# Second layer: expert weights kept in SBUF, eight row buffers for nine, shared places for short tiles

## The chip, the cores and the metric

The kernel runs on one core of a Trainium2 chip. The metric is the device time of one execution in microseconds (us), the median over several runs. Engines are named as in the profile: PE (matmul) with PEld (its weight loads), DVE (vector), ACT (scalar), POOL (GpSimd) and SP (used here as a queue for DMAs).

## The reference

A graph network of two layers on 3125 nodes of 256 features and 100000 edges sorted by destination. Each layer adds to `x` a neighbour part and an attention part, then an expert part. The change concerns the second layer, which is this:

```python
xn = _layernorm(x, axis=-1)
x = x + _L1_gnn_ref(xn, W, attn_src, attn_dst, edge_index, edge_type) + _L1_mix_ref(xn[None], ...)[0]
x = x + _L1_ffn_ref(_layernorm(x, axis=-1)[None], ...)[0]

# _L1_gnn_ref: 8 relations, 8 heads of 32
h_all = einsum('nf,rof->rno', x, W).reshape(r, n, h, d)
h_src = h_all[edge_type, src]; h_dst = h_all[edge_type, dst]
scores = leaky_relu(h_src . attn_src + h_dst . attn_dst, 0.2)
w = exp(scores - max(segment_max(scores, dst), 0)[dst])
w = w / (segment_sum(w, dst) + 1e-12)[dst]
out = segment_sum(h_src * w, dst)

# _L1_mix_ref: k, v normalized per head
kv = einsum('bhsd,bhse->bhde', k, v) / S
out = (q @ kv) @ wo.T + bo

# _L1_ffn_ref: 6 experts of three 256x256 layers, the two best per node
rh = relu(f @ router_w1 + router_b1); p = softmax(rh @ router_w2 + router_b2)
h1 = relu(f @ expert_w1 + b1); h2 = relu(h1 @ expert_w2 + b2); y = h2 @ expert_w3 + b3
out = sum over the two best of softmax weight * y
```

## The kernel before

Everything up to about 1500 us is the first layer and is not touched. Then come two stages of the second layer.

**The table stage** (L2263 to L2361, about 1504 to 1788 us): for each of 25 tiles of 128 nodes, the rows `y` of the first layer's experts are gathered, the node is normalized, and its products with the weights of all 8 relations are written to a table in DRAM (`tab`, rows of 264 numbers: 256 features and 8 scores); `kv` is summed up on the side. The loads of this stage are issued by SP at its start: `wq`, `wo` and `bo` of the attention part, then `wt` (2 MB), `wkv` and smaller ones.

**The attention and expert stage** (class `Layer1`, 1787 us to the end) has one order of work written out by hand: the instructions of each engine run in the order of the program (`manual_schedule`). The edges are cut into 25 blocks, 24 of 34 x 128 edges and one of 15 x 128. `run` goes through them:

- `gather(b)` fetches the table rows of a block into row tiles `r` of 7 edges per partition, five tiles a block (7, 7, 7, 7, 6), by one indirect DMA of POOL per edge column (L1383). The tiles come from the pool `at_r`, which has nine buffers: a tile takes the place of the one nine before it, when PE has summed that one.
- `start(b)` issues the place data (`a3`, `mk`, `m4` on ACT's queue, in `places`) and the edge lists `oe`, five chunks of 256 KB (on SP's queue, `load`), compares a chunk into one-hots `ot` on DVE (`turn`, L1203), and picks the destination scores by matmul (`pick`, L1214); `own` (L1225) reduces them on DVE. This is done for block b+2 at the end of block b and spread through block b+1. `oe` and `ot` have three buffers each.
- `block(b)` adds the scores (`raw`, L1402; it needs all five row tiles), takes the maximum over a node's edges by scans (DVE, with a transpose `lp` on PE, a copy `ls` on ACT, L1417, and the way back), the exponential on ACT (L1444), then for each row tile multiplies rows by weights on DVE (L1454), builds the one-hots `oh` (L1457) and sums by matmul (`sums`, L1468). The sum of a block is closed in the next block (`close`, L1486 and on), normalized and turned into `xt` for the experts.
- The experts work on groups of blocks (`TOGETHER`: five groups of four, one of three, one of two). A group's work is a generator, `group`, whose units PE, ACT and DVE take piece by piece at set points of a block (`take(us)`). The three weights of each expert are loaded in every group again, a few experts ahead, by SP (`weights` through `load_k`, L352), into tiles with two buffers for each of the three layers:

```python
for i, n in ((1, e + 2), (2, e + 2), (3, e + 1)):
    self.weights(ws, i, n)
```

- `mix`, ahead of block 0, makes one matrix of `kv`, `wq` and `wo` and adds the attention part to all 25 tiles, reading back the normalized nodes (`xt`, 512 KB a load, two buffers, L1554).

What a queue holds is served in order: an issue on SP that waits for a free place holds up all that SP issues later.

Of the kernel before, what the change touches and what calls it, by code (L numbers as in the profile page):

```python
# [7 lines left out]
F32 = mybir.dt.float32  # L8
BF = mybir.dt.bfloat16
# [4 lines left out]
PSUM = bass.MemoryType.PSUM  # L14
DRAM = bass.MemoryType.DRAM

N, D, E = 3125, 256, 100000
P = 128
# [15 lines left out]
NE1 = 6  # L34
R, HD, DH = 8, 8, 32
# [872 lines left out]
CW = 8  # L908
# [226 lines left out]
class Layer1:  # L1135
# [3 lines left out]

    def __init__(self, tc, C, a, out, one, wk, rows, ps, B, table, apart, x1t, mixed, xs):  # L1140
        self.tc, self.nc, self.C, self.a, self.out = tc, tc.nc, C, a, out
        self.one, self.wk, self.rows, self.ps = one, wk, rows, ps
        self.B, self.table, self.apart, self.xs = B, table, apart, xs
        self.x1t, self.mixed = x1t, mixed
        nc = tc.nc
        t = lambda shape, dt, name: one.tile(shape, dt, name=name)
        self.ones = t([1, P], F32, "l1_ones")
        nc.vector.memset(self.ones, 1.0)
        self.carry = [t([HD, 2, P], F32, f"carry{i}") for i in range(2)]
        for x in self.carry:  # L1150
            nc.vector.memset(x, -BIG)
        self.down = t([P, NE1], F32, "l1_down")
        nc.vector.tensor_scalar(self.down, C.row[:, :NE1], -1.0, float(NE1), op0=OP.mult, op1=OP.add)
        ld = lambda shape, name, src: (t(shape, F32, name), src)
        loads = [ld([NE1, D], "b3", a["L1_ffn_expert_b3"]),
                 ld([P, NE1, 2], "bc1", a["L1_ffn_expert_b1c"]), ld([P, NE1, 2], "bc2", a["L1_ffn_expert_b2c"]),
                 ld([P, NE1], "rw2", a["L1_ffn_router_w2"]), ld([P, 1], "rb1", a["L1_ffn_router_b1c"]),
                 ld([P, NE1], "rb2", row_bc(a["L1_ffn_router_b2"], NE1))]
        for x, src in loads:
            nc.sync.dma_start(x, src)  # L1160
        self.b3, self.bc1, self.bc2, self.rw2, self.rb1, self.rb2 = (x for x, _ in loads)
        self.rw1 = load_k(nc, one, a["L1_ffn_router_w1"], "rw1")
        self.late = []
        self.stores = []
        self.units = iter(())
        self.queue = []
# [19 lines left out]
    def load(self, A, c):  # L1186

        if c >= A["n"]:
            return
        k = min(CW, A["w"] - c * CW)  # L1190
        i = A["c0"] + c * CW
        oe = self.wk.tile([P, CW * P], BF, name="oe", bufs=3)
        self.nc.sync.dma_start(oe[:, :k * P], self.B.order[i:i + k, :].rearrange("c e -> (c e)")[None, :]
                               .to_broadcast([P, k * P]))
        A["oe"][c] = oe

    def turn(self, A, c):

        if c >= A["n"]:
            return  # L1200
        k = min(CW, A["w"] - c * CW) * P
        ot = self.wk.tile([P, CW * P], BF, name="ot", bufs=3)
        self.nc.vector.tensor_scalar(ot[:, :k], A["oe"].pop(c)[:, :k], self.C.p, None, op0=OP.is_equal)  # L1203
        A["ot"][c] = ot
# [13 lines left out]
    def own(self, A, c):  # L1218
        nc = self.nc
        if c >= A["n"]:  # L1220
            return
        k = min(CW, A["w"] - c * CW)
        s = slice(c * CW, c * CW + k)
        own = self.wk.tile([P, CW, HD, R], F32, name="own")
        nc.vector.tensor_tensor(own[:, :k], A["dp"].pop(c)[:, :k],  # L1225
                                A["orel"][:, s, None, :].to_broadcast([P, k, HD, R]), OP.mult)
        nc.vector.tensor_reduce(A["ad"][:, s, :], own[:, :k], AX.X, OP.add)  # L1227
# [17 lines left out]

    def weights(self, ws, i, e):
        if e < NE1:
            ws[i, e] = load_k(self.nc, self.wk, self.a[f"L1_ffn_expert_w{i}"][e], f"ew{i}")

    def group(self, t0, nt, xt):  # L1250
# [4 lines left out]
        bc = lambda x: x[:, :, None].to_broadcast(sh)  # L1255
        ws = {}
        for i, e in ((1, 0), (1, 1), (2, 0), (3, 0), (2, 1)):
            self.weights(ws, i, e)

        rp = ps.tile([P, 512], F32, name="hp", bufs=2)  # L1260
        for j in range(2):
            nc.tensor.matmul(rp[:, :W], self.rw1[:, j, :], xt[:, j, :W], start=(j == 0), stop=(j == 1))  # L1262
        rh = wk.tile([P, 512], F32, name="rh", bufs=1)
        nc.scalar.activation(rh[:, :W], rp[:, :W], AF.Relu, bias=self.rb1)
# [10 lines left out]
        h1, h2 = {}, {}  # L1275
# [68 lines left out]
        for e in range(NE1):  # L1344
# [9 lines left out]
            for i in range(nt):  # L1354
# [4 lines left out]
                yield 0.9  # L1359
            for i, n in ((1, e + 2), (2, e + 2), (3, e + 1)):  # L1360
                self.weights(ws, i, n)
            self.store()
# [27 lines left out]
    def block(self, b, part, A, N):  # L1390
# [3 lines left out]
        mk, m4 = A["mk"], A["m4"]  # L1394
        keep = wk.tile([P, 2, HD, w + 2], F32, name="kp", tag=f"kp{w}", bufs=1)
        for i in range(2):
# [4 lines left out]
        for s0, k, r, _ in part:  # L1401
            nc.vector.tensor_tensor(raw[:, s0:s0 + k, :], A["ad"][:, s0:s0 + k, :], r[:, :k, D:], OP.add)  # L1402
        sc = wk.tile([P, HD, w + 2], F32, name="sc", tag=f"sc{w}")
        inner = sc[:, :, 1:w + 1]
# [3 lines left out]
        for i in range(2):  # L1408
            t = wk.tile([P, HD, w], F32, name="tm", tag=f"tm{w}", bufs=1)
            nc.vector.tensor_tensor(t, inner, m4[:, 3 - i, None, :w].to_broadcast([P, HD, w]), OP.add)  # L1410
            nc.vector.tensor_reduce(lf[:, i, :], t, AX.X, OP.max)
# [23 lines left out]

        mx = wk.tile([P, 2, HD, w + 2], F32, name="mx", tag=f"mx{w}", bufs=1)
        f = lambda x: x.rearrange("p h c -> p (h c)")
# [14 lines left out]
        for q, (s0, k, r, got) in enumerate(part):  # L1452
# [3 lines left out]
            i = c0 + s0  # L1456
# [21 lines left out]
    def close(self):  # L1478
# [8 lines left out]
        nc.vector.reciprocal(den, den)  # L1487
        y = wk.tile([P, HD, DH], F32, name="y")
        nc.vector.tensor_tensor(y, sp[:, :D].rearrange("p (h d) -> p h d", h=HD),
# [40 lines left out]
    def mix(self):  # L1530

        nc, wk, ps, xs = self.nc, self.wk, self.ps, self.xs
        cx, wq, wo, bo = self.mixed
        ct = wk.tile([P, 2, P], F32, name="ct", tag="x1")
# [43 lines left out]
    def run(self):  # L1578
# [10 lines left out]
        for b in range(NB):  # L1589
            ahead = self.gather(b + 1) if b + 1 < NB else None  # L1590
            self.block(b, part, A, N)
            part, A = ahead, N
            N = self.start(b + 2) if b + 2 < NB else {"n": 0}
            self.store()
# [480 lines left out]
def fast(ctx: ExitStack, tc: tile.TileContext, a, out, flag):  # L2075
# [192 lines left out]
    with tc.tile_pool(name="n1", bufs=1) as n1:  # L2268
        apart = dram.tile([NB, P, 3, HD * R], BF, name="apart")
        x1t = dram.tile([(NB + 3) // 4, P, 2, 512], F32, name="x1t")  # L2270
        cx = n1.tile([P, 2, P], F32, name="cx1")
        wq = load_k(nc, n1, a["L1_mix_wqT"], "wq")
        wo = load_k(nc, n1, a["L1_mix_woT"], "wo")
        bo = n1.tile([1, D], F32, name="bo")
# [89 lines left out]
        with tc.tile_pool(name="at_1", bufs=1) as one, tc.tile_pool(name="at_w", bufs=2) as wk, \  # L2364
                tc.tile_pool(name="at_r", bufs=9) as rows, tc.tile_pool(name="at_p", bufs=1, space=PSUM) as ps:
            with tc.manual_schedule():
                Layer1(tc, C, a, out, one, wk, rows, ps, B_, tab2, apart, x1t, (cx, wq, wo, bo), xs).run()

# [60 lines left out]
```

## Time and profile before

| what | value |
|---|---|
| time, median of 3 runs | 3158.33 us (3147.89 to 3163.19) |
| the profiled execution | 3159.71 us, span 3157.9 us |
| busy: PE, DVE, POOL, ACT | 83%, 56%, 35%, 23% of the span |
| mean granted clock of PE | 0.907 |
| row gathers, L1383 | 831, 1105 ns each |
| `sums` matmuls, L1468 | 1662, 411 ns each |
| row multiplications, L1454 | 123, 1953 ns each |
| loads of expert weights, L352 | 126 of 256 KB |
| loads of edge lists, L1193 | 97 of 256 KB, 25 shorter |
| HBM read, written | 321.04 MB, 97.96 MB |

How to read it: shares of busy time are means over stages with different limits. A line such as "POOL r L1383 <- PE tp L1524: 25.4, 5, 8.9" in the list of waits says that POOL's instructions of line 1383, which write tile `r`, waited for that PE instruction 25.4 us in total, 5 times, 8.9 us at the longest. In a timeline each row is: start in us, length in us, engine, line, operation, what it writes and reads, shapes, how many; in the bracket, the idle time of the engine before it and what ended that. An engine's name with a q (SPq, ACTq) is its queue issuing a DMA. A releaser is inferred: the instruction named came last before the start.

### The profile page before, as it was taken

How to read it: one execution, taken by the hardware profiler on the slowest of the kernel's cores; microseconds unless marked ns; L12 is line 12 of the kernel's file. 1: busy time of each engine (PE TensorE's matmuls, PEld its weight loads, DVE VectorE, ACT ScalarE, POOL GpSimd, SP SyncE). 2: the span in 40 equal slices, each digit the busy share in tenths (PEclk: the TensorE clock that was granted, in tenths of full speed). 3: DMA queues.
4: the chain of work that ended last, by engine and by line, in shares of the span. 5: the costliest groups of instructions: out<-in, count | busy, mean ns of one | idle time of the engine just before them, and what ended most of it. 6: DMA issues, size and time to landing. Idle time of an engine off the chain costs nothing. (4 is left out here: it accounts for less than half of the span.)

```text
span 3157.9 us, 38213 instructions
## 1 busy us (share of the span) xinstructions
PE 2610.1 (83%) x13696; PEld 1774.8 (56%) x13696; DVE 1752.6 (56%) x3882; ACT 737.6 (23%) x1637; POOL 1113.6 (35%) x1040
## 2 busy tenths in 40 slices
PE   2667789999992999999699785397887877878878
PEld 1455544454562888888344354355555555555656
DVE  7777754444664111111676557566777667766652
ACT  3333402212231222222222101122121222212122
POOL 2000000001116500000600267777777777767700
PEclk9887999999995999999899887689898898898989
DMA  3555432223323665645643444445555555545512
GB/s 110 148 154 158 125 93 73 74 77 95 109 81 96 203 195 186 200 148 168 192 132 128 146 139 121 137 139 146 142 147 146 141 141 146 148 127 155 147 40 85
DMA packets 382415, 421.68 MB, mean 134 GB/s; under 512 B 143879, under 2 KB 316045, under 8 KB 381959
## 3 DMA queue, kind: packets, MB, share of 16 engines
q1 hardware_dynamic: 311680, 270.61, 28.5%
q0 software_dynamic: 49072, 132.49, 14.9%
q10 hardware_dynamic: 21462, 16.03, 1.7%
q8 instruction: 110, 1.80, 0.2%
q14 instruction: 91, 0.74, 0.1%
HBM read 321.04 MB, written 97.96 MB: 133 GB/s over the span
## 5 line engine op out<-in xcount | busy, mean ns | idle before, releaser
L1383 POOL DMA_INDIRECT r<-tab,b_at x831 | 918.6, 1105 | 498.5 <-issue 230.9
L1468 PE MATMUL sums<-r,oh 128*128 128x264 f32 x1662 | 423.6, 411 | 43.3 <-DVE oh L1457 24.8
L1468 PEld LDWEIGHTS sums<-r,oh 128*128 128x128 f32 x1662 | 334.1, 203 | 126.4 <-issue 50.7
L1909 POOL DMA_INDIRECT route_x<-x,slot x50 | 50.3, 1007 | 869.2 <-DVE slot L1905 722.8
L1454 DVE TENSOR_TENSOR r<-r 128x1792 f32<-128x1792 f32 (+2 forms) x123 | 240.2, 1953 | 0.0
L2184 PE MATMUL agg<-at,px 128*128 128x512 bf16 (+2 forms) x1050 | 237.4, 357 | 2.2 <-DMA at<-adj 2.2
L2030 PE MATMUL fhp<-fxe,fw 128*128 128x256 f32 x1024 | 233.9, 387 | 0.8 <-DVE fxe L2015 0.6
L2038 PE MATMUL fyp<-fw,fhid 128*128 128x256 f32 x1024 | 226.3, 379 | 0.0
L1322 PE MATMUL yp<-ew,h 128*128 128x256 f32 x600 | 163.8, 424 | 68.9 <-DVE xs L1326 68.9
L2184 PE MATMUL agg<-at,py 128*128 128x512 bf16 (+4 forms) x1200 | 216.4, 333 | 0.0
L2030 PEld LDWEIGHTS fhp<-fxe,fw 128*128 128x128 f32 x1024 | 188.1, 193 | 40.7 <-ACT fhid L2031 6.3
L2301 POOL DMA_INDIRECT y<-route_y,slot x50 | 50.3, 1005 | 452.9 <-DMA wq<-in_L_mix_wqT 429.0
L2038 PEld LDWEIGHTS fyp<-fw,fhid 128*128 128x128 f32 x1024 | 192.1, 190 | 24.8
L1273 ACT ACTIVATE h<-hp,bc 128x512 f32<-128x512 f32 (+2 forms) x168 | 106.2, 639 | 421.4 <-PE hp L1270 421.4
L2320 PE MATMUL hp<-wt,xt 128*128 128x512 f32 x400 | 183.3, 607 | 8.9 <-DVE stage L2323 5.6
L2031 ACT ACTIVATE fhid<-fhp,fb 128x256 f32<-128x256 f32 x256 | 121.1, 473 | 290.8 <-PE fhp L2030 267.2
L1322 PEld LDWEIGHTS yp<-ew,h 128*128 128x128 f32 x600 | 122.3, 213 | 105.7 <-DVE xs L1326 81.6
L1214 PE MATMUL dp<-a,ot 128*128 128x64 bf16 x2493 | 109.1, 206 | 82.5 <-DVE own L1225 45.9
L1634 PE MATMUL cnt<-oh_s,oh_a 128*125 128x128 bf16 x1250 | 99.3, 240 | 88.2 <-ACT adj_o L1635 60.6
L1270 PE MATMUL hp<-xt,ew 128*128 128x512 f32 (+2 forms) x336 | 158.3, 597 | 13.9 <-ACT h L1273 12.3
L1634 PEld LDWEIGHTS <-oh_a 128*125 128x125 bf16 x1250 | 96.1, 155 | 125.7 <-issue 75.2
L1214 PEld LDWEIGHTS <-ot 128*128 128x128 bf16 x2493 | 104.0, 106 | 104.7 <-issue 48.6
(418 smaller groups left out, 3858.6 us busy)
## 6 DMA issues: line engine op xcount, KB each, us to landing
fw<-in_L_ffn_W SPq DMA_DIRECT2D x64, 1024.0 KB
ew<-in_L_ffn_expert_w SPq DMA_DIRECT2D x126, 256.0 KB
at<-adj SPq DMA_DIRECT2D x44, 640.0 KB
route_x<-zero SPq DMA_DIRECT2D x104, 256.0 KB
tab<-stage SPq DMA_DIRECT2D x25, 1056.0 KB
oe<-b_order SPq DMA_DIRECT2D x97, 256.0 KB
adj<-adj_o SPq DMA_DIRECT2D x78, 250.0 KB
r<-tab,b_at POOLq DMA_INDIRECT x831
```

Source lines behind the costliest of these rows:

```text
L1214: nc.tensor.matmul(dp[:, i, :, :].rearrange("p h r -> p (h r)"), ot[:, i * P:(i + 1) * P], A["a3"][:, j, :], start=(j == 0), stop=(j == 2))
L1270: nc.tensor.matmul(hp[:, :W], ws[i, e][:, n, j * P:(j + 1) * P], x[:, n, :W], start=(n == 0), stop=(n == 1))
L1322: nc.tensor.matmul(yp, h2[e][:, n, i * P:(i + 1) * P], ws[3, e][:, n, :], start=(n == 0), stop=(n == 1))
L1383: st = self.nc.gpsimd.indirect_dma_start(out=r[:, c, :], out_offset=None, in_=self.table, in_offset=bass.IndirectOffsetOnAxis(ap=self.B.at ...
L1454: nc.vector.tensor_tensor(rv, rv, r[:, :k, D:, None].to_broadcast([P, k, HD, DH]), OP.mult)
L1468: mm = nc.tensor.matmul(self.sums, oh[:, c, :], r[:, c, :], start=(i == 0), stop=(i == w - 1))
L1634: nc.tensor.matmul(cnt[:, i, :], a[:, o, :M], s[:, o, :], start=(h == 0), stop=(h == 1))
L2030: nc.tensor.matmul(hp, w1[:, k, i * P:(i + 1) * P], xe[:, k, :], start=(k == 0), stop=(k == 1))
L2031: nc.scalar.activation(hid[:, i, :], hp, AF.Gelu, bias=b1[:, 0, i:i + 1])
L2038: nc.tensor.matmul(yp, hid[:, i, t * P:(t + 1) * P], w2[:, i, :], start=(i == 0), stop=(i == K1 - 1))
L2184: nc.tensor.matmul(agg[g][:, :cw], parts[j][:n, k, g * P:(g + 1) * P], at[:n, i, :cw], start=(k == 0 and j == 0), stop=(k == NB - 1 and j ...
L2320: nc.tensor.matmul(hp.rearrange("p r d -> p (r d)"), xt[:, k, :], wt[:, k, j * 512:(j + 1) * 512], start=(k == 0), stop=(k == 1))
```

## The change

- The weights of the six experts (18 tiles of 256 KB, 2 KB a partition) get places of their own in the pool of single buffers (`at_1`) and are loaded once: two experts after each of blocks 0, 1 and 2. `group` only reads them, and `weights` is gone.
- The row pool `at_r` has eight buffers for nine. `oe` and `ot` have two for three, `own` and `y` one for two.
- The tiles `kp`, `sc`, `tm` and `mx`, which had places apart for the short last block, use those of the full blocks; `rh` takes a place of `h2`.
- `wq` and `wo` are no longer loaded with the table stage's weights but at the start of `Layer1`, into the two places of `xt`; the constant `l1_ones` is replaced by a row of one that exists.

```diff
-        self.ones = t([1, P], F32, "l1_ones")
-        nc.vector.memset(self.ones, 1.0)
+        self.ones = ones[:1, :]
...
         self.rw1 = load_k(nc, one, a["L1_ffn_router_w1"], "rw1")
+        self.wq, self.wo = (wk.tile([P, 2, D], F32, name=n, tag="xt") for n in ("wq", "wo"))
+        for x, n in ((self.wq, "wq"), (self.wo, "wo")):
+            nc.sync.dma_start(x, a[f"L1_mix_{n}T"].rearrange("(k p) n -> p k n", p=P))
+        self.ws = {}
...
-        oe = self.wk.tile([P, CW * P], BF, name="oe", bufs=3)
+        oe = self.wk.tile([P, CW * P], BF, name="oe", bufs=2)
...
-        ot = self.wk.tile([P, CW * P], BF, name="ot", bufs=3)
+        ot = self.wk.tile([P, CW * P], BF, name="ot", bufs=2)
...
-        own = self.wk.tile([P, CW, HD, R], F32, name="own")
+        own = self.wk.tile([P, CW, HD, R], F32, name="own", bufs=1)
...
-    def weights(self, ws, i, e):
-        if e < NE1:
-            ws[i, e] = load_k(self.nc, self.wk, self.a[f"L1_ffn_expert_w{i}"][e], f"ew{i}")
-
     def group(self, t0, nt, xt):
...
-        ws = {}
-        for i, e in ((1, 0), (1, 1), (2, 0), (3, 0), (2, 1)):
-            self.weights(ws, i, e)
+        ws = self.ws
...
-        rh = wk.tile([P, 512], F32, name="rh", bufs=1)
+        rh = wk.tile([P, 2, 512], F32, name="rh", tag="h2")[:, 0, :]
...
-            for i, n in ((1, e + 2), (2, e + 2), (3, e + 1)):
-                self.weights(ws, i, n)
             self.store()
...
-        keep = wk.tile([P, 2, HD, w + 2], F32, name="kp", tag=f"kp{w}", bufs=1)
+        keep = wk.tile([P, 2, HD, w + 2], F32, name="kp", bufs=1)
...
-        sc = wk.tile([P, HD, w + 2], F32, name="sc", tag=f"sc{w}")
+        sc = wk.tile([P, HD, w + 2], F32, name="sc")
...
-            t = wk.tile([P, HD, w], F32, name="tm", tag=f"tm{w}", bufs=1)
+            t = wk.tile([P, HD, w], F32, name="tm", bufs=1)
...
-        mx = wk.tile([P, 2, HD, w + 2], F32, name="mx", tag=f"mx{w}", bufs=1)
+        mx = wk.tile([P, 2, HD, w + 2], F32, name="mx", bufs=1)
...
-        y = wk.tile([P, HD, DH], F32, name="y")
+        y = wk.tile([P, HD, DH], F32, name="y", bufs=1)
...
-        cx, wq, wo, bo = self.mixed
+        (cx, bo), wq, wo = self.mixed, self.wq, self.wo
...
             self.block(b, part, A, N)
+            for e in range(2 * b, min(2 * b + 2, NE1)):
+                for i in (1, 2, 3):
+                    self.ws[i, e] = load_k(self.nc, self.one, self.a[f"L1_ffn_expert_w{i}"][e], f"ew{i}_{e}")
             part, A = ahead, N
             N = self.start(b + 2) if b + 2 < NB else {"n": 0}
...
-        wq = load_k(nc, n1, a["L1_mix_wqT"], "wq")
-        wo = load_k(nc, n1, a["L1_mix_woT"], "wo")
         bo = n1.tile([1, D], F32, name="bo")
...
-                tc.tile_pool(name="at_r", bufs=9) as rows, tc.tile_pool(name="at_p", bufs=1, space=PSUM) as ps:
+                tc.tile_pool(name="at_r", bufs=8) as rows, tc.tile_pool(name="at_p", bufs=1, space=PSUM) as ps:
             with tc.manual_schedule():
-                Layer1(tc, C, a, out, one, wk, rows, ps, B_, tab2, apart, x1t, (cx, wq, wo, bo), xs).run()
+                Layer1(tc, C, a, out, one, wk, rows, ps, B_, tab2, apart, x1t, (cx, bo), T_.ones, xs).run()
```

More of the change, by code (lines that the diff above doesn't have):

```diff
@@ L1135, with __init__ @@
 class Layer1:
-    def __init__(self, tc, C, a, out, one, wk, rows, ps, B, table, apart, x1t, mixed, xs):
+    def __init__(self, tc, C, a, out, one, wk, rows, ps, B, table, apart, x1t, mixed, ones, xs):
         self.tc, self.nc, self.C, self.a, self.out = tc, tc.nc, C, a, out
```

## The prediction

> **What bounds the kernel now.** The change touches the last stage, from 1787 us on, so I read that stage alone. First the slices of the page:
>
> ```profile
> POOL 2000000001116500000600267777777777767700
> PEclk9887999999995999999899887689898898898989
> ```
>
> POOL is about 75% busy from the 24th to the 38th of the 40 slices: that is the gather of table rows (L1383), 831 instructions with a mean of 1.105 us. The list of waits for POOL, from 2000 to 3010 us:
>
> ```profile
> POOL r L1383 <- issue: 188.9, 620, 0.3
> POOL r L1383 <- PE tp L1524: 25.4, 5, 8.9
> ```
>
> The 0.3 us in front of each gather is its issue. So a gather costs at least 1.25 us, one of 34 edges 42.5 us, and POOL truly waits only 25.4 us in 1010. Next the waits of DVE (1890 to 3000 us) and of SP (from 1900 us on):
>
> ```profile
> DVE raw L1402 <- DMA r<-tab,b_at: 44.9, 7, 10.0
> DVE run L1421 <- ACT ls L1417: 41.5, 14, 5.3
> DVE ot L1203 <- DMA oe<-b_order: 40.2, 10, 7.2
> ```
>
> ```profile
> SPq L1193 <- DVE ot L1203: 576.0, 62, 22.7
> SPq L352 <- PE yp L1322: 275.8, 30, 25.1
> SPq L352 <- PE hp L1270: 199.6, 21, 25.0
> ```
>
> SP's queue stands for 475 us behind weight loads (L352) that wait for PE to free their places, and the edge lists (`oe`, L1193) behind them come late to DVE. The timeline puts the blocks in order. The start of the first row addition of a block (DVE L1402) comes at 2435.4, 2479.9, 2535.2, 2592.9 and 2634.2 us for blocks 12 to 16, then again every 199 us: four blocks make a cycle, since four blocks fill one expert group, whose work then runs inside the next three blocks. POOL waits once in a cycle, for the row buffer that the block without expert work frees late:
>
> ```profile
> 2616.40 0.95 POOL L1383 DMA_INDIRECT r<-tab,b_at  x1 [0.30 <-issue]
> 2621.76 0.94 POOL L1383 DMA_INDIRECT r<-tab,b_at  x1 [4.42 <-PE tp L1524]
> ```
>
> Block 16's last row tile (2621.76) starts when block 15's first is summed (2621.5): tile t waits for tile t-9. The stage is thus a loop, gather → block → freed buffer → gather, and DVE and PE carry most of it: only the second block of a cycle waits for its gather (5.0 us). What DVE and PE do where block 15 begins, in the timeline of each (the bracket is the idle time before, and what ended it):
>
> ```profile
> 2591.00 0.72 DVE L1203 TENSOR_SCALAR ot<-oe,p 128x1024 bf16<-128x1024 bf16 x1 [6.23 <-DMA oe<-b_order]
> ```
>
> ```profile
> 2588.23 2.83 PE L1468 MATMUL sums<-r,oh 128*128 128x264 f32 x12
> 2593.47 0.86 PE L1214 MATMUL dp<-a,ot 128*128 128x64 bf16 x24 [2.40 <-DMA a<-apart]
> ```
>
> DVE loses 6.23 us to a late list, and PE stands too, but PE's last reason is another one.
>
> **The change, part by part.** Each number here is a shift of an event against the trace.
>
> *Start.* `wq` and `wo` now come in the SP queue just before the edge lists of block 0, and `xt` may only load into their places once PE has read them. A 256 KB load takes 3.2 to 5.4 us from issue to landing in the chain (`oe` 3.22, `ew` 5.38). Two of them ahead of the first list (5.1 us from issue, 1791.97, to use, 1797.1) add 2 to 5 us. The first `xt` (512 KB) can be issued at about 1816.3, when `wq` is transposed (last read ends 1816.2); at 5 to 7 us it lands at 1821 to 1823, against a use at 1818.4: 3 to 5 us. Together 5 to 10; I take 7, and 3 as the low end if the first loads overlap. The Trainium skill ("DMA: Bandwidth & Descriptors", section "Anatomy of one DMA — SWDGE (gpsimd) path") fits a transfer as 2.0 us and its bytes at 436 GB/s, for POOL's queue; by it `xt` would take 3.2 us and cost about 2 less than I take, an estimate.
>
> *Eight row buffers.* Tile t now waits for t-8: of a block's five tiles the fourth, not the fifth, needs the block before. At the start POOL stands from 1855.4 instead of 1864.4 until block 0 frees its first tile (1880.4, now +7); then it has 13 gathers to issue for block 1, not 6: 7 more, 8.75 us free of DVE, 11.3 in the slowest tiles beside the multiplications L1454. I take 10: **+17** at block 1. Blocks 2 to 4 are bound by the gather (DVE waits 14 to 15 us there), so the +17 stays. In each later cycle the tile that is added behind the late release is the fourth of blocks 8, 12, 16, 20: it took 9.9, 9.5, 9.4, 8.7 us: **+9.4** a cycle. The skill ("SBUF — State Buffer", section "Who interferes with whom") lets a DVE instruction with two SBUF inputs contend with GpSimd only where that reads SBUF, and infers that descriptor writing is not held up; the rows differ, gathers beside L1454 take up to 2.70 us instead of 0.95. By the rule the tile would cost 8.75.
>
> *Weights kept.* 126 loads become 18, six after each of blocks 0 to 2. They are issued behind the last list load of the next block, at about the start of the message stage, into free memory; 1.5 MB at 150 GB/s (what the queues move now) is 10 us, and the lists behind them are needed some 25 us later: nothing, or up to 10 us once if that cover fails. What is won: (a) the list wait at L1203, in blocks 7, 11, 15, 19, 23: 7.5, 8.6, 6.9, 8.5, 8.7 us. But PE can't move up that far: its sums end at 2591.06, and its next matmul needs `a` from ACT's queue, issued at 2588.57 behind the ReLU of the last layer and landed after 4.9 us, at the same time as the lists; alone I give it 2.5 to 3. So the matmul starts at about 2591.2, not 2593.47, the wait of 1.16 for DVE behind it goes too, and where the layer behind it ran slow after the pause (3.66 us against 1.88 in block 11, at a granted clock of 0.57 from 2394 to 2398 us) 1.8 more. Over the five blocks that gives 4.2, 4.6, 3.5, 4.7, 5.0: **-4.4** a cycle (bounds -1.8 and -8.5). (b) Block 5, 9, 13, 17, 21 see their last row 3.8 to 4.2 us after its gather, beside five or six weight loads; blocks 2 to 4, without them, 1.9 to 2.0: **-2** a cycle (0 to -2.2). (c) PE's own waits for `ew`: 0.5, 0.2, 0.7 in three cycles: **-0.3**. The tail from 3050 us on shows no wait for a weight: nothing.
>
> *Two buffers for `oe` and `ot`, one for `own` and `y`, shared places.* `own` and `y` are written and read by DVE in order; `ot` of chunk 3 needs the matmuls of chunk 1, which DVE already awaits through `own`; `oe` of chunk 2 is now loaded after the compare of chunk 0, some 8 us ahead of use in the shortest block, against 3.2 to 4.4 us of landing. `rh` in a place of `h2` waits for sums that PE has done before. Only block 24 has the other width, and its places are free a block earlier. Nothing, as long as the lists land; otherwise the same 1 to 2 us per block, once a cycle.
>
> *Table stage.* 512 KB fewer lie ahead of the 2 MB of `wt` and the first `y` rows (8.8 us from gather to use at 1515.75, the rest of them 2 to 4): **-2** (0 to -4).
>
> **The sum.** +17 at block 1; four cycles (to the gathers of blocks 8, 12, 16, 20) of +9.4 - 2 - 4.4 - 0.3 = +2.7: +11; from block 21 to the end once more -2 - 4.4 - 0.3 = -7; table -2: **+19**. The profiled execution took 3159.71 us (span 3157.9, 1.8 around it), and would be 3179; against the median of 3158.33 I predict **3177 us**, 0.6% slower. A difference of 0.5% (15.8 us) is about what a measurement of this kernel can tell from none.
>
> **Rivals.** *No change that can be told* (0.28): PE does follow DVE's full gain, since `a` lands early. Then a cycle is 9.4 - 2 - 7.7 - 0.3 = -0.6, the end -10: 17 - 2.4 - 10 - 2 = +3, 3161 us. For it: DVE's wait is on the critical chain at 2587.17 and 2591.75. Against it: the 2.40 us that PE waits for `a` by itself.
>
> *Faster* (0.15), one mechanism: the gathers that are now pushed behind the late release fall where DVE stands, and run at 1.25 us. Place: the fourth and fifth tile of blocks 8, 12, 16, 20. They took 19.1 us in block 16; free of DVE they take 16.3: -2.8 a cycle, on top of the full list wait. 17 + 4(-3.4) - 10 - 2 = -9; with the start at 13 instead of 17 and the list wait at its longest (8.7) in all cycles -18: 3140 us. It decides if a cycle falls under 194 us (now 199).
>
> *Clearly slower, within the forecast's side:* `a` lands as late as now (gain 1.8) and the last row also (0): a cycle is +7.3, the end -2, the start 20: +47, 3205 us. That the weights are not kept can be excluded: `ws` is filled once and `group` loads nothing.
>
> **How the numbers follow.** Forecast 0.57, no change 0.28, faster 0.15. The range reaches from the middle between the second rival and the first (3150) to near the worst case (3200). Alone, the forecast's cases lie from 3168 to 3205.
>
> **What would show it.** 18 `ew` loads, none beside PE in steps of a cycle; no DVE wait for `oe` in blocks 7 to 23; POOL standing from 1855 to about 1888; four waits of 5 to 9 us for the first sums of blocks 7, 11, 15, 19, now before the fourth tile of the next block; DVE waiting about 5 to 8 us for rows in blocks 8, 12, 16, 20; a cycle of 201 to 203 us; the tail from block 24 unchanged (113 us). I am wrong if the cycle is 196 or less, or if block 0's first sums stay at 1880.

## The result, and the profile after

| | before | after |
|---|---|---|
| median of 15 runs, us | 3151.08 (3142.01 to 3163.19) | 3162.23 (3158.00 to 3169.49) |
| after / before | | 1.0031, 95% interval 1.0019 to 1.0043 |
| profiled execution, us (span) | 3159.71 (3157.9) | 3158.0 (3156.2) |

The change costs 11 us (6 to 14 by the interval). The forecast was +19. Here and below, an execution more than 1.5% above the fastest of its kernel is left out. The profiled execution of after happens to be no longer than that of before, because its stages ahead of the change ran 8 us faster in that execution. So I compare the stage by itself: from the first row gather to the end it takes 1371.1 us before and 1380.7 us after (1775.5 to 3156.2), **+9.6**. The table stage, from the first `y` row to the first row gather, went from 279.9 to 276.9 us, -3.0.

The slices of after's page show POOL as full as before in the stage:

```profile
POOL 2000000001116400000600357777777777777700
PEclk9888999999996999999899787699898898998998
```

POOL's list of waits from 2000 to 3010 us (time in all, how often, longest):

```profile
POOL r L1378 <- issue: 182.5, 598, 0.6
POOL r L1378 <- PE tp L1519: 22.8, 11, 4.4
```

It stands for a buffer eleven times and not five, but not for longer in all: three waits of 4.4 us and four of 1.7 to 2.0 (before, four of 4.4 to 8.9), the rest no longer than an issue. DVE (1890 to 3000 us) no longer waits for a list at all; it waits for rows more than twice as long:

```profile
DVE raw L1397 <- DMA r<-tab,b_at: 106.3, 19, 8.0
...
DVE run L1416 <- ACT ls L1412: 48.2, 15, 4.4
```

SP (1900 to 3010 us) is no longer behind weights. It stands because it runs far ahead, with the next list waiting for its place:

```profile
SPq L1196 <- DVE ot L1206: 913.7, 82, 20.2
...
SPq L1196 <- DMA ew<-in_L_ffn_expert_w: 4.3, 2, 2.3
```

At the start, POOL's timeline has one long wait, before the fourth tile of block 1 and no longer the fifth:

```profile
1871.64 1.81 POOL L1378 DMA_INDIRECT r<-tab,b_at  x1 [26.99 <-PE sums L1463]
```

In the loop it now stands before a fourth tile. This is block 16, in which before had the same 4.42 us at the fifth:

```profile
2611.33 0.94 POOL L1378 DMA_INDIRECT r<-tab,b_at  x1 [0.30 <-issue]
2616.69 0.94 POOL L1378 DMA_INDIRECT r<-tab,b_at  x1 [4.42 <-PE tp L1519]
```

And where block 15 begins, PE goes from the sums straight into the matmul of the next edges, which has no wait in front of it any more:

```profile
2587.47 2.83 PE L1463 MATMUL sums<-r,oh 128*128 128x264 f32 x12
2590.14 0.86 PE L1217 MATMUL dp<-a,ot 128*128 128x64 bf16 x24
```

### The profile page after: what moved, and what is told of

It is laid out like the page before. It is cut to its first block, busy times and chain, and to the rows that moved or that the text cites. A ratio compares the mean times of both kernels' runs of the same rounds, so it can differ in the third digit from the quotient of the medians.

```text
span 3156.2 us, 37950 instructions
## 1 busy us (share of the span) xinstructions
PE 2576.6 (82%) x13652; PEld 1754.8 (56%) x13696; DVE 1749.1 (55%) x3881; ACT 738.7 (23%) x1637; POOL 1126.1 (36%) x1040
## 4 chain that ended last, share of the span: by engine, by line
PE 57%; DVE 14%; POOL 7%; SPq 7%; DMA 6%; issue 6%; ACT 2%; DVEq 0%; ACTq 0%; POOLq 0%
PE agg L2182 12%; PE fhp L2028 7%; PE fyp L2036 7%; SPq L1816 6%; POOL r L1378 6%; PE sums L1463 6%; PE hp L2316 5%; PE hp L1267 5%; PE yp L1319 4%; DMA r<-tab,b_at 3%; DVE r L1449 2%; PE hp L2202 2%; PE kvp L2334 1%; DVE oh L1452 1%; PE deg L2186 1%
## 5 line engine op out<-in xcount | busy, mean ns | idle before, releaser
L1378 POOL DMA_INDIRECT r<-tab,b_at x831 | 931.0, 1120 | 505.0 <-issue 222.8
L1463 PE MATMUL sums<-r,oh 128*128 128x264 f32 x1662 | 408.7, 400 | 43.2 <-DVE oh L1452 24.7
L1463 PEld LDWEIGHTS sums<-r,oh 128*128 128x128 f32 x1662 | 324.1, 197 | 121.5 <-issue 50.7
L2182 PE MATMUL agg<-at,py 128*128 128x512 bf16 (+5 forms) x1181 | 215.7, 334 | 0.9
L1319 PE MATMUL yp<-ew,h 128*128 128x256 f32 x600 | 155.2, 408 | 72.8 <-DVE xs L1323 72.2
L2182 PEld LDWEIGHTS <-py 128*128 128x128 bf16 (+1 forms) x1200 | 111.4, 99 | 88.7 <-issue 5.5
```

The lines of the kernel that those rows point to most:

```text
L1319: nc.tensor.matmul(yp, h2[e][:, n, i * P:(i + 1) * P], ws[3, e][:, n, :], start=(n == 0), stop=(n == 1))
L1378: st = self.nc.gpsimd.indirect_dma_start(out=r[:, c, :], out_offset=None, in_=self.table, in_offset=bass.IndirectOffsetOnAxis(ap=self.B.at ...
L1463: mm = nc.tensor.matmul(self.sums, oh[:, c, :], r[:, c, :], start=(i == 0), stop=(i == w - 1))
L2182: nc.tensor.matmul(agg[g][:, :cw], parts[j][:n, k, g * P:(g + 1) * P], at[:n, i, :cw], start=(k == 0 and j == 0), stop=(k == NB - 1 and j ...
```

## The experiments

They ran later, on three chips, and on each of them the kernel before took 3715 to 3747 us, not 3151. All ratios below are against the kernel before on the same chip, in the same series of runs. This second condition became half of the study, since there the change has the other sign. What takes longer there can be read from the traces (below). Why it does, no run tells; the record does not name the chip of the first result, so it is not known whether the chip is what differs.

**One row buffer less, alone** (twice).

```diff
-                tc.tile_pool(name="at_r", bufs=9) as rows, ...
+                tc.tile_pool(name="at_r", bufs=8) as rows, ...
```

> The kernel before with eight row buffers, nothing else changed. Loop theory (gather, block, freed buffer, gather): block 1 comes 9 to 10 us later at the start, and each of the four cycles to block 20 gets 9.4 us longer, the tile that moves behind the late release: 9.5 + 4 x 9.4 = +47 us against the kernel before, cycles of 208 us, and POOL waits 10 us before the fourth tile of blocks 8, 12, 16 and 20. Rival (POOL's own rate sets the stage and its buffers don't): only the start, +10 us, and cycles of 199.

> The kernel before with eight row buffers and nothing else changed. Loop theory, where the kernel before takes about 3150 us: the first gathers stand from tile (1,3) on, +10 at block 1, and the fourth tile of each cycle's second block is gathered behind the late release, +7 to +10 in each of five cycles, with nothing that pays for it: +35 to +50 us, ratio 1.011 to 1.016. Rival (the buffer costs only at the start, and the change lost its time elsewhere): +10 to +15, ratio 1.003 to 1.005. Where the kernel before takes about 3750 us: 0.998 again.

Measured: 0.9984 (0.9967 to 1.0001) and 1.0008 (0.9989 to 1.0027). Neither price was there: in this condition the buffer is free.

**Kept weights with nine row buffers.** To make room, three experts' weights serve all six.

```diff
+            for e in range(2 * b, min(2 * b + 2, NE1 // 2)):
...
+                    self.ws[i, e + 3] = self.ws[i, e]
```

> The changed kernel with nine row buffers. To make room only the weights of experts 0 to 2 are kept, and experts 3 to 5 use them as well; the number of instructions of PE, DVE, ACT and POOL is that of the changed kernel. Loop theory: without the eighth buffer's limit the saved list waits and landings count in full until POOL's rate binds: 27 us faster than the kernel before (3.1% of nothing else is needed), so some 37 us faster than the change, cycles of 194 to 196 us. Rival (the change is slower because of its start and the later loads, not its ring): within 10 us of the changed kernel, cycles near 201.

Measured: 0.9952 (0.9926 to 0.9977). The gain has the predicted sign, and is smaller than the theory's 27 us. It is level with that of the changed kernel in this condition (0.996, below), which is what the rival had.

**The weight loads one expert later, all else as before.** SP then stands less behind loads.

```diff
-        for i, e in ((1, 0), (1, 1), (2, 0), (3, 0), (2, 1)):
+        for i, e in ((1, 0), (1, 1), (2, 0)):
...
-            for i, n in ((1, e + 2), (2, e + 2), (3, e + 1)):
+            for i, n in ((1, e + 2), (2, e + 1), (3, e)):
```

> The kernel before with its 126 weight loads, issued one expert later in the program, so that the place that each needs is free when SP comes to it: w1 of expert e+2, w2 of e+1 and w3 of e behind expert e. Nothing else is changed. If SP's standing behind weight loads is what made the edge lists late, the waits at L1203 in blocks 7 to 23 fall from 7 to 9 us to under 2, PE's matmul behind them waits for the place data only, and a cycle is some 5 us shorter: 20 to 25 us faster in all. Rival (the lists are late because the weight traffic fills the queues): no change within 5 us, the waits stay above 4 us.

Measured: 0.9972 (0.9954 to 0.9990). SP stands 209 us behind weight loads (L352) in its trace, and 563 us in the trace of the kernel before further down. So shorter standing alone gives part of what kept weights give. How large a part, the two intervals do not tell, nor what the bytes have to do with it.

**Late streamed loads with eleven row buffers** (twice): after's layout, its weights streamed again in the late order, `bufs=11`.

> The changed kernel with the weights loaded again in every group, two places for each of the three layers, issued one expert later as in the run before; the room that this frees goes to eleven row buffers. Loop theory: no list waits, and no row wait either after the start: 42 to 47 us faster than the kernel before, cycles of 193 to 195 us, bound by POOL's gathers. Rival (traffic of the weights slows the landings and the place data enough to matter): 25 us or less faster, with waits of DVE for rows of 4 us after each gather.

> The changed kernel with its weights streamed again, in two places for each layer, each load issued one expert later than in the kernel before, so that SP hardly stands; the room holds eleven row buffers. Loop theory, where the kernel before takes about 3150 us: the list wait is gone as in the changed kernel and three more row buffers carry POOL over the late release: -30 to -50 us, ratio 0.984 to 0.990. Rival (after eight buffers POOL has nothing to gain, and the 126 loads beside the rows cost what they cost before): 0.997 to 1.002. Where the kernel before takes about 3750 us: 1.006 again.

Measured: 1.0063 (1.0044 to 1.0082) and 1.0059 (1.0036 to 1.0083). The loop theory's gain of 42 to 47 us, expected in the first run, turned into a loss of 23; the second expected 1.006 for this condition.

**The changed kernel itself.**

> The changed kernel once more, since the first four experiments ran on a chip where the kernel before takes 3747 us and not 3151. Loop theory (the lost row buffer costs at the start and in each cycle, and the kept weights give nearly as much back): 1.002 to 1.005 of the kernel before where that takes about 3150 us. Where it takes about 3750 us, the traces of the first four experiments show that POOL has issued all the rows it has buffers for long before the blocks need them (it waits for the release of a tile in nearly every block, 3 to 29 us each time), and the blocks wait for a result of PE instead; there the row buffer costs nothing and only the kept weights count: 0.994 to 0.999, like the 0.995 of the kernel with kept weights and nine row buffers.

Measured: 0.996 (0.9941 to 0.9979). So the same program is 11 us slower than before in the first condition and 12 to 15 us faster in the second.

What differs can be read at one place. ACT's timeline in block 4, first of after's trace in the first condition, then of the same program in the second (start, duration; in the bracket the idle time before it and what ended it, where "remote" stands for a signal whose sender the trace doesn't tell):

```profile
2042.12 0.17 ACT L1425 COPY sc<-cp 128x8 f32<-128x8 f32 x1 [1.82 <-PE cp L1424]
```

```profile
2236.69 0.17 ACT L1425 COPY sc<-cp 128x8 f32<-128x8 f32 x1 [25.09 <-remote]
```

The copy waits for two small transposes, which by their modelled end PE had done 23.3 us earlier in the second trace:

```profile
2213.00 0.38 PE L1424 MATMUL cp<-ident,carry 8*128 8x8 f32 x2 [0.19 <-issue]
2240.00 1.44 PE L1217 MATMUL dp<-a,ot 128*128 128x64 bf16 x24 [26.62 <-DVE own L1228]
```

POOL in the same stretch: the last gather of its run, and then a long wait for a buffer:

```profile
2231.67 0.95 POOL L1378 DMA_INDIRECT r<-tab,b_at  x1 [0.30 <-issue]
2248.85 2.67 POOL L1378 DMA_INDIRECT r<-tab,b_at  x1 [16.24 <-PE tp L1519]
```

ACT goes on 4.1 us after POOL's last gather has ended. I call a signal of PE held when the next update of PE's semaphore in the trace comes more than 3 us after the modelled end of the matmul that sends it, and add up these stretches, overlapping ones once. In the first condition that gives 6 us (before) and 0 (after); in the second 656 us in this trace, in 63 stretches. Of these, 62 lie beside a run of indirect DMAs; 28 end within 5.5 us after a run's end, 34 while a run goes on. Of 442 signals that PE sends inside such runs, 153 are held, of the 1419 others one. The totals are rough: 64 of 1861 updates of PE are missing in this trace, and the same count gives 455 us for DVE, of whose 3634 updates 414 are missing, though DVE's signals are in time, as the next figures show.

The copy itself gives a check without these records. From the modelled end of the transposes to its start it is under 0.1 us in all 25 blocks in both traces of the first condition. In this trace it is 200 us in all, over 3 us in 12 blocks and 23.3 at the most. The other way, PE's transposes start within 0.15 us of the DVE result (`carry`) that they need, in all 25 blocks, in both conditions.

The granted clock is a rival: over the stage it is 0.776 here and 0.872 in the first condition. But PE is busy only 78 us longer in the stage, and the stage is 473 us longer (1853.7 against 1380.6). Most of that is PE standing, 733 us against 338. Outside the stage it costs too: from the end of the first layer's aggregation to the second layer of its experts, beside POOL's indirect DMAs, it takes 124 us instead of 74.

A buffer that is free there fits this. POOL stands for buffers 429 us in the same trace (from 1890 to 3450 us), since the blocks that free them are late:

```profile
POOL r L1378 <- PE tp L1519: 429.2, 21, 26.9
```

**The kernel before, for its trace.**

> The kernel before, unchanged, for its trace beside those of the others. Where it takes about 3720 us: theory of the held signals: PE's signals held for 650 to 760 us in all, as in the other traces, POOL standing for a buffer in nearly every block (10 us and more), so that a row buffer more or less is free. Rival (the rows come late there): DVE waits for the rows instead, and POOL hardly stands.

Measured: 765 us held, and POOL standing 20 times for a buffer, as the theory of the held signals says:

```profile
POOL r L1383 <- PE tp L1524: 444.2, 20, 29.0
```

**Nine row buffers and two layers of weights kept, the third streamed through three places.**

```diff
+    def third(self, e):
+        if e < NE1:
+            w = self.wk.tile([P, 2, D], F32, name="ew3", bufs=3)
+            self.nc.sync.dma_start(w, ...)
+            self.ws[3, e] = w
...
+        self.third(0)
...
+            self.third(e + 1)
...
-                for i in (1, 2, 3):
+                for i in (1, 2):
```

> The changed kernel with the weights of the first two layers kept (12 places) and those of the third streamed through three places, each load issued a whole expert ahead of its use and behind a place that is long free, so that SP does not stand; that leaves room for nine row buffers. Loop theory, where the kernel before takes about 3150 us: what the kept weights give without the price of the buffer, -20 to -30 us, ratio 0.990 to 0.994. Rival (the list wait that is removed only turns into waits of POOL and PE elsewhere): 0.998 to 1.002. Where the kernel before takes about 3750 us: 0.995, like the kernel with all weights kept and nine row buffers.

Measured: 0.9961 (0.9939 to 0.9983), level with the changed kernel. Together with the runs above: in the second condition keeping weights is worth 0.4 to 0.5% with eight or nine buffers, and a buffer nothing.

**Seven and five row buffers** (`bufs=7`, `bufs=5` in the changed kernel).

> The changed kernel with seven row buffers in place of eight. Loop theory, where the kernel before takes about 3150 us: the third tile of a block now waits for the block before, +155 to +165 us, ratio 1.05. Where it takes about 3720 us, the traces show PE's signals held back for 650 us in all, always while POOL writes a run of gathers, and let go about 4 us after the run ends. By that (theory of the held signals) a shorter lead of POOL costs nothing, since the block waits for the end of the run and not for the row, and shorter runs let PE go earlier: 0.985 to 1.000. Rival (POOL is the bound there as well): 1.03 to 1.05.

> The changed kernel with five row buffers: the rows of a block are only gathered as those of the block before are summed. Loop theory, where the kernel before takes about 3150 us: gather and block hardly overlap, +400 to +700 us, ratio 1.13 to 1.22. Where it takes about 3720 us, by the theory of the held signals: POOL's runs are cut into single tiles of seven gathers (8.8 us), each behind a release by PE, so that PE is held for less than the 26 us of now in each block; what is won there and what is lost in overlap are of one size, 0.97 to 1.05. Rival (POOL is the bound): 1.13 and more.

Measured: 0.997 (0.9947 to 0.9992) and 1.032 (1.0291 to 1.035); held 557 and 433 us. Both lie where the theory of the held signals put them, though its range for five buffers (0.97 to 1.05) was wide, and the rivals (1.03 and more, 1.13 and more) are out.

**Late streamed loads with nine buffers** (`bufs=9` in place of 11).

> The kernel with weights streamed one expert later, now with nine row buffers and not eleven. Where the kernel before takes about 3720 us: theory of the held signals (longer runs of gathers hold PE longer, and that is what the eleven buffers lost): 0.996 to 1.000, under the 1.006 of eleven. Rival (the streamed loads in the changed kernel's layout lose it): 1.004 to 1.008. Where it takes about 3150 us: loop theory, 0.992 to 0.994.

Measured: 1.0005 (0.9987 to 1.0023), just above the theory's range. So the 1.006 goes with the two buffers more, not with the streamed loads. How they lose it stays open: the held time is no larger with eleven buffers (691 and 655 us, against 740 here, on another chip), so the theory's reason, longer holding, is not shown.

**Pauses on POOL**, after each row tile, or after the second and fourth only.

```diff
             part.append((s, k, r, got))
+            if s // RW in (1, 3):
+                idle = self.wk.tile([P, 512], I32, name="idle", bufs=1)
+                for _ in range(8):
+                    self.nc.gpsimd.iota(idle, pattern=[[1, 512]], base=0, channel_multiplier=0)
```

> The changed kernel with POOL kept away from gathers for some 4.5 us after each row tile (eight iotas of 512 numbers into a place that nobody reads). Where the kernel before takes about 3720 us, theory of the held signals: a run is now 7 gathers (8.8 us) and PE is let go in each pause, so that the 26 us of holding in a block shrink by half or more: held signals 250 to 400 us in all (650 without pauses), and the time falls to 0.93 to 0.98 though POOL does 22 us more work in a block. Rival (PE is held by something else, or the holding simply goes on): held as before, and POOL's extra work makes it 1.00 to 1.05. Where it takes about 3150 us: POOL becomes the bound in all blocks, 1.12 to 1.16.

> The same with a pause after the second and the fourth tile of a block alone: runs of up to 14 gathers (17.5 us). Theory of the held signals: between the kernel without pauses and the one with five of them, 400 to 550 us held, 0.96 to 0.99. Rival: 0.996 to 1.02. Where the kernel before takes about 3150 us: 1.03 to 1.06.

Measured: 0.993 (0.9908 to 0.9952) with five pauses, 277 us held; **0.9608** (0.9583 to 0.9632) with two, 537 us held. With two pauses POOL does 9 us more in a block, computes nothing new by it, and the kernel is 147 us faster than the kernel before. That is the test of the cause: with pauses in the runs of gathers PE is held less. ACT's copy, which was late by 200 us in all, is late by 111 us with two pauses and by 42 with five, at the same granted clock over the stage (0.777 in both, 0.776 without). Whether it is POOL's writing of descriptors that holds PE or the transfers, which a pause thins out as well, is not told apart. With five pauses the gain is nearly gone, against the 0.93 to 0.98 expected. There I had not reckoned with the next bound: 42.5 us of gathers and five pauses of 4.5 us are 65 us a block without any slow gather (72 us in the trace, 69 in the changed kernel's), POOL no longer stands for buffers, and DVE waits for rows instead:

```profile
DVE raw L1400 <- DMA r<-tab,b_at: 523.5, 50, 13.5
```

**The same pauses in the kernel before, and in the one with two layers kept** (14 iotas of 240 numbers, for lack of room).

> The kernel before (streamed weights, nine row buffers) with POOL kept away from gathers for some 4.5 us after the second and the fourth row tile of a block (14 iotas of 240 numbers). Where it takes about 3745 us without them: if what the runs of gathers do is the same for all kernels and a row buffer stays free, the kept weights' 0.4% is what separates it from the changed kernel with pauses: 0.963 to 0.968. If the row buffer's price comes back as PE is held less, it is level with the changed kernel with pauses or ahead of it: 0.950 to 0.961. Where it takes about 3150 us: 1.03 to 1.06.

> The kernel with the weights of two layers kept, those of the third streamed, and nine row buffers, with the same pauses. If a row buffer stays free: like the changed kernel with pauses, 0.957 to 0.964. If its price comes back: 0.945 to 0.957. Where the kernel before takes about 3150 us: 1.02 to 1.05.

Measured: 0.9556 (0.9491 to 0.9621) and **0.952** (0.9472 to 0.9568), 444 us held in the second. The second is clear of the changed kernel with pauses (0.9608) and the first is not. The two are not clear of each other: by the medians they are 177 and 169 us faster than the kernel before on their own chip. So with less holding, nine buffers seem to be worth something again, 0.9% in the kernel with two layers kept. (It ran on another chip than the changed kernel with pauses, so this is a hint and not a proof.) POOL's wait for buffers says the same, 164 us with eight buffers and pauses, then 83 us with nine:

```profile
POOL r L1378 <- PE tp L1523: 164.3, 19, 19.5
```

```profile
POOL r L1386 <- PE tp L1531: 83.1, 8, 13.5
```

The kernel with two layers kept, nine buffers and pauses has the lowest ratio in the second condition. In the first it was not run; POOL has no 9 us to spare in a block there (42.5 us of gathers in a block of 50).

**The changed kernel without row multiplications**, to see who slows the gather.

```diff
-            nc.vector.tensor_tensor(rv, rv, r[:, :k, D:, None].to_broadcast([P, k, HD, DH]), OP.mult)
```

> The changed kernel without the row multiplications (DVE L1449), so its rows are summed unweighted. What is asked is who slows the gather. Theory (a multiplication with both inputs in SBUF holds up POOL's descriptors): the mean of a gather falls by what lies beside L1449, from 1120 to about 995 ns where the kernel before takes about 3150 us, from 1032 to about 980 where it takes about 3720; the extra time that is left lies beside the one-hots. Rival (descriptor writing is not held up by DVE, and the extra time comes from the DMA queues): the mean stays within 15 ns of 1120 or 1032.

The group of gathers on the pages of the changed kernel in both conditions, and of this one (instructions, busy time, mean ns of one; idle time before, and what ended most of it):

```profile
L1378 POOL DMA_INDIRECT r<-tab,b_at x831 | 931.0, 1120 | 505.0 <-issue 222.8
```

```profile
L1378 POOL DMA_INDIRECT r<-tab,b_at x831 | 857.9, 1032 | 1040.7 <-PE tp L1519 447.4
```

```profile
L1378 POOL DMA_INDIRECT r<-tab,b_at x831 | 812.3, 977 | 993.5 <-ACT xt L1520 378.1
```

From 1032 to 977 ns, with 980 expected; one run took 3596.8 us, against 3720 of the kernel before. In the first of the three traces, 127 of the 146 us by which gathers exceed 945 ns lie in the 190 gathers that overlap a multiplication. So the multiplications do hold up the gathers. The Trainium skill's inference that descriptor writing is not held up by DVE ("SBUF — State Buffer", section "Who interferes with whom") doesn't agree with this, unless what is held up is the gather's reading of its row numbers (`b_at`) from SBUF; no run here separates the two.

## Why the prediction was right and wrong

The forecast was for the first condition, and no experiment ran there. What follows rests on the two traces of it, one execution each, aligned at the first gather; the experiments of the second condition bear on single terms only. "First sums" stands for the end of the sums of a block's first row tile.

| term | predicted | measured |
|---|---|---|
| start, before the rows of block 1 | +7 | +2.3 |
| more gathers behind the first release | +10 | +9.5 |
| blocks 2 to 4 | 0 | -2.0 |
| the fourth tile, each of four cycles (the gather's end of blocks 8, 12, 16, 20 against those first sums) | +9.4 | +10.7, +9.5, +9.5, +9.5 |
| weights kept, each of four cycles (first sums of blocks 7, 11, 15, 19 against the gather's end of blocks 4, 8, 12, 16) | -6.7 | -9.6, -7.2, -7.0, -8.8 |
| from block 20's rows to the end | -7 | -6.8 |
| table stage | -2 | -3.0 |
| sum | +19 | +6.6 in the traces, +11 in the medians |

*Right.* The mechanism: a loop in which tile t now waits for tile t-8, so that the fourth tile is gathered behind the late release; that the list waits would go and pay back most of it; DVE's 7.7 us of waiting for rows in blocks 8, 12, 16 and 20 (5 to 8 predicted). Three of the four cycles came as long as predicted: between the gathers' ends of blocks 4, 8, 12, 16 and 20 it is 198.0, 201.5, 201.4 and 201.2 us, where 201 to 203 were predicted and 196.9 to 200.5 stood before.

*Right by luck: the price of the tile.* 9.4 us was what the fourth tile took in its old place. In the new one, beside the multiplications, it takes 11.35 us (block 16; 9.15 before), and the fifth, now past them, 7.27 instead of 9.41. The two errors cancel, and +9.5 is left. In block 8 POOL does not stand for the release at all, so the +10.7 there has another make-up.

*Mis-sized: the start.* The step "together 5 to 10; I take 7" failed in both halves; 2.3 was measured. The two loads ahead of the lists delay the first list's use by 1.9 us: it comes 12.2 us after the first gather instead of 10.3, just under the low end of 2. And PE does not wait for `xt`, where I took 3 to 5 us. The first `xt` took the place of `wo`, not of `wq`: it is issued when PE's last read of `wo` ends, 1.6 us ahead of the last read of `wq`. It landed at 1808.68, 3.3 us after its issue instead of 5 to 7, ahead of its use:

```profile
1803.24 2.07 PE L1534 MATMUL yp<-wo,ct 128*128 128x256 f32 x4 [0.46 <-ACT ct L1561]
1805.35 1.90 SPq L1549 DMA_DIRECT2D xt<-x1t  x2
1809.29 1.32 PE L1553 MATMUL yp<-m,xt 128*128 128x256 f32 x4
```

The times that I borrowed were of loads that shared SP's queue with others: while the `ew` load of 256 KB took its 5.38 us, that queue moved 0.78 MB. In the 3.3 us of `xt` it moved 0.54 MB, little besides `xt` itself; gathers moved another 0.29 MB. The skill's fit for a transfer on POOL's queue ("DMA: Bandwidth & Descriptors", section "Anatomy of one DMA — SWDGE (gpsimd) path"), which the prediction set aside, gives 3.2 us as an estimate and would have been nearer.

*Mis-sized: the weights kept.* -6.7 a cycle was taken, and -8.1 is the mean of the four. The step on `a` was right: it lands 1.7 to 2.8 us after its issue in blocks 7, 11, 15 and 23 (2.5 to 3 taken; 4.8 to 6.3 before, beside the late lists), and PE's matmul follows the sums after 0 to 0.3 us. It is still issued as far ahead of the end of the sums as before, 2.5 us:

```profile
2588.57 0.33 ACTq L1174 DMA_DIRECT2D a<-apart  x1
```

```profile
2587.76 0.33 ACTq L1177 DMA_DIRECT2D a<-apart  x1
```

What was too small is the gain behind it. From the first sums of block 6, 10, 14 and 18 to those of the next block the cycles win 5.7, 5.8, 4.3 and 5.5 us, where the prediction had 4.2, 4.6, 3.5 and 4.7. Part of the difference is work of PE behind the pause that now runs faster and that the sum left out (`yp`, 6.77 instead of 7.17 us in block 15, 6.74 instead of 7.62 in block 11). The part of the cycle up to those first sums wins 2.8 us on average, where -2 and -0.3 were put. So the condition of the rival "no change that can be told" did come true, `a` lands early. But its 7.7 us did not: DVE's first row addition of blocks 7, 11, 15 and 19 moves up by 7.4 to 8.8 us against those first sums of the block before, and then DVE waits 2.1 to 4.0 us for the rows of the fifth tile. Had I put -8.1 and 2.3 in the sum, it would have been 12.3 + 4(9.4 - 8.1) - 7 - 2, +8.5.

*Not foreseen.* The wait behind the late release was 4.4 us in blocks 12, 16 and 20, under the 5 to 9 predicted, and there was none in block 8, where POOL itself is late. POOL stood 27 us at the start, not 33. It waited four more times, 1.7 to 2.0 us, before the fourth tiles of blocks 10, 14, 18 and 22. Blocks 2 to 4 were gathered in 144.4 us instead of 146.4, with no wait for a buffer in either trace. The tail is 3.1 us longer (116.7 us from block 24's last row addition to the end, 113.5 before). The granted clock was a half in some 20 us of it, before in some 16; one execution of each is too little to tell if that belongs to the change. And the base: three runs had given 3158 us for the kernel before, fifteen give 3151.

*The second condition.* The prediction knew one bound, POOL's gathers, and its price of a buffer follows from it. Where PE's signals are held, the bound is another one, and the terms come out one by one as that says: the buffer 0 instead of +48 us (10 at the start and 9.4 in each of four cycles), the weights -15 us instead of -34 (five times 6.7), and the sign turns.

## What to carry to other kernels

Price a buffer of a ring by who stands for whom: where the producer is the bound, the tile that falls behind the late release costs its time in each cycle (9.5 us here, by one pair of traces); where the producer stands anyway, a buffer is free, and the same change has the other sign. Take a tile's time from the place where it will run, not from where it ran. When a wait is removed and a second one lies behind it, ask what the second one takes alone, and then what the work behind both gains. And before trusting a trace for a term of 5 us at a stage's edge, look which buffer is free first, and whether the duration that you borrow was taken in a queue that other loads shared.

## What was not expected of the hardware

In the second condition signals of PE reached ACT late, by up to 23 us at the copy of `sc` in the changed kernel's trace (and by up to 53 us by the records of semaphore updates, some of which are missing). By these records it is so in all 17 traces, on three chips, nearly always beside runs of indirect DMAs on POOL (62 of 63 times in that one). DVE's own signals in the same stretch came in time: in the trace of the kernel before with eight buffers, DVE's updates are there at 2219 to 2221 us, beside PE's that are held from 2219 to 2240 us. With two pauses of 4.5 us in each block of gathers the changed kernel goes from 0.996 to 0.961 of the kernel before on the same chip, and PE is held less, which shows the runs as the cause. Whether it is the matmul or only its signal that waits, and why the first condition shows nothing of it, stays open: matmul ends are modelled in these records, and no run could bring the first condition back.

A gather with no DVE instruction beside it takes 945 ns in both conditions; beside the multiplication of rows, whose two inputs lie in SBUF, up to 2.75 us (before, first condition). Over all 831 gathers the multiplications cost 55 ns each in the second condition (1032 to 977, one trace each).
